# A graph layer with eight splits of the edges instead of six, and a reordered opening

## The chip, the cores and the metric

The kernel runs on one core of a Trainium2 chip. The profile names the core's engines: PE (TensorE, matrix products; PEld is its weight loading), DVE (VectorE), ACT (ScalarE), POOL (GpSimd) and SP (SyncE, which issues most transfers). Each engine runs its own instructions in the program's order and waits for the others by semaphores. The metric is device time in microseconds, from the first to the last instruction with what lies around them, median of the runs.

## The reference

One layer of message passing over 100,000 edges and 6,250 nodes, 128 features. `src` is random, `dst` is sorted.

```python
row, col = (edge_index[0], edge_index[1])          # src, dst
msg_in = jnp.concatenate([x[row], x[col], edge_attr], axis=-1)
h = msg_in @ W + b                                  # W: (384, 128)
mu = jnp.mean(h, axis=-1, keepdims=True)
var = jnp.mean(jnp.square(h - mu), axis=-1, keepdims=True)
h = (h - mu) * jax.lax.rsqrt(var + LN_EPS) * gamma + beta
msg = jax.nn.relu(h)
out = jax.ops.segment_sum(msg, row, num_segments=x.shape[0])
...
x = _layernorm(x + out, axis=-1)
```

## The kernel before

**Two passes, woven together.** Edges are worked in 782 tiles of 128, four tiles to a block (196 blocks, `q`). The first pass makes, for each edge, `edge_attr @ W[2D:]` (`features`, L943) plus the projected `x[dst]`, picked by a one-hot product from a window of 42 rows (`edges`, L960; the one-hot is `ohd`, L932). ACT copies the block from PSUM to `hs` and appends each edge's place in its node block (`evict`, L968 and L969, one L969 for each block). Then POOL scatters the rows into DRAM, one indirect DMA for each tile (`scatters`, L990), sorted by node block: node `n` belongs to block `n % 50`. Where a row goes is ranked by `places` on DVE and PE (L685 to L731, products L725) ahead of time.

**Splits.** The 782 tiles are cut into splits, each with its own DRAM tensor `sorted_d[s]` and a fixed room for each node block: `SPLITS` says (tiles, tiles of room for a node block, rows of the room that are never cleared, pieces in which it is ranked). What the scatters may leave empty is cleared by DMAs from `empty` ahead (`clear`, L431). Once a split is complete, the second pass reads it back by pairs of node blocks (`load_pair`, L1049 before). A pair of a split with room `k` has 2k *slots* (tiles of 128 sorted rows).

**What a pair does** (class `Pair`): a one-hot of the nodes (`ones`, L1106, DVE), its transposes (`turn`, PE L1118, copied by ACT in `turned`), the rows put into PSUM (`seed`), the node's own projection added by products (`pick`, L1145), squares and root (`square`, ACT L1154 and L1157), reciprocal and `msg` on DVE (`root` L1163, `scale` L1169: one `msg` instruction for each slot), the sum over edges by products into `pa` (`sums`, L1178), and the addition to `acc` (`add`, L1196). While tiles are still coming, the loop over blocks does a few pair steps in each (`work`, table `FLOW`); how many is set by `due`, which spreads a split's 25 pairs, four steps each, evenly over the blocks from its completion (plus `LAG`) to the next.

**The end.** The pairs of the last split (called x) can start only after the last scatter, and they also finish the nodes (`Finish`: the outer layer norm and the store). The order of steps there comes from a planner, `in_order`, a list scheduler with a table of ranks (`RANK`) and of ready times (`READY`) in its own units. To have less left, 8 of the 25 x pairs are halved: their first tiles of both node blocks are worked earlier, two pairs at a time, as four *units* (`UNITS`, class `Unit`, loads L1062, sums L1214, additions L1221). Before the change the units' rows lay in the last split's tensor: its first 68 tiles (`FULL`) had to be scattered, and `check_full` tested that these fill the first tile of each node block.

Of the kernel before, what the change touches and what calls it, by code (L numbers as in the profile page):

```python
# [8 lines left out]
F32 = mybir.dt.float32  # L9
# [4 lines left out]
ALU = mybir.AluOpType  # L14
# [71 lines left out]
def flat(t):  # L86
# [4 lines left out]
READY = {"u": 13.5, "x": 25.5, "pool": 24.5}  # L91
RANK = {"O": -1.5, "T": 0.4, "U": -3.2, "S": 0.3, "K": 4.4, "Q": 6.1, "R": -2.7, "V": 4.1, "C":
        7.1, "M": 9.0, "A": 8.9, "B": 10.6, "St": 12.6, "FQ": 15.6, "W": 9.5, "E": 25.4, "L":
        -13.2, "F": -6.8, "D": 14.0, "N": 1.9, "H": 5.3}
PACE = 2.6
LOOK = 0.04
# [30 lines left out]
def last_steps(old, units, halves, n):  # L127
# [42 lines left out]
    for i in range(n):  # L170
# [15 lines left out]
        steps["V", "x", i] = Step("DVE", 0.107, 0.09, [("R", "x", i)], rank("V"))  # L186
# [5 lines left out]
        if i == n - 1:  # L192
            last_pair(steps, i, ring, rank)
            continue
# [3 lines left out]
                                  takes=("y",) if i < n - 3 else (), gives=((("F", "x", i), "xs"),))  # L198
# [9 lines left out]
        if i == n - 2:  # L208
            steps["E0", "x", i] = Step("DVE", 0.3, 0.1, [("W", "x", i)], rank("E"))
            steps["E1", "x", i] = Step("ACT", 0.5, 0.1, [("W", "x", i)], rank("E"))  # L210
        else:
            steps["E", "x", i] = Step("POOL", 0.88, 0.06, [("W", "x", i)], rank("E"))
        if i < n - 3:
            steps["D", "x", i] = Step("SP", 0.4, 2.5, [("E", "x", i)], rank("D"),
# [4 lines left out]
def last_pair(steps, i, ring, rank):  # L219
# [4 lines left out]
    steps["N", "x", i] = Step("PE", 1.5, 0.2, [("H", "x", i), ("O", "x", i)], rank("N"),  # L224
# [82 lines left out]
def fast_path(ctx, tc, io, bad_d):  # L307
# [177 lines left out]
    def first_nodes(t0, t1):  # L485
        c = slice(t0, t1)
        nc.vector.tensor_scalar(sloc[:, c], src_i[:, c], 0.5, 1.0 / NB, op0=ALU.add, op1=ALU.mult)
        nc.vector.tensor_scalar(sloc[:, c], sloc[:, c], -0.5, MAGIC, op0=ALU.add, op1=ALU.add)
# [184 lines left out]
    def places(s, t0, T):  # L673
# [59 lines left out]
        if t0 + T == first_tile[-2] + FULL:  # L733
            check_full()
        yield

    def check_full():

        n = place_pool.tile([P, NB], F32, name="n_edges")
        nc.vector.tensor_scalar(n, room[-1], P - 1.5, None, op0=ALU.is_lt)  # L740
        red = place_pool.tile([P, 1], F32, name="red")
        nc.vector.tensor_reduce(red, n.unsqueeze(1), axis=AX.X, op=ALU.max)
        nc.vector.tensor_tensor(bad[:, 2:3], bad[:, 2:3], red, op=ALU.add)
# [122 lines left out]
    def edge_loads(q):  # L866
# [7 lines left out]
        for n in ([(0, g)] if q else [(i, 1) for i in range(g)]):  # L874
            c0, c1 = n[0] * PT * P, min((n[0] + n[1]) * PT * P, (TILES - t0) * P)
            nc.sync.dma_start(eT[:, c0:c1], io["eT"][:, t0 * P + c0:t0 * P + c1])
            if q == 0 and n[0] == 0:
                load_first(0)
                load_first(1)
                load_x(0, 1)  # L880
# [94 lines left out]
    full_scatters = []  # L975
# [3 lines left out]
    def scatters(n, tied):  # L979
# [7 lines left out]
        for k, (s, q, j) in enumerate(waiting[:n]):  # L987
# [8 lines left out]
            if first_tile[-2] <= t < first_tile[-2] + FULL:  # L996
                full_scatters.append(i.ins.name)
# [4 lines left out]
            if t >= first_tile[-2] + FULL:  # L1002
                tc.declare_no_dep(i.ins, group="halves", reason="see check_full")
                tc.add_to_no_dep_group("behind", i.ins)
# [39 lines left out]

    def load_pair(s, p):
# [3 lines left out]
        nc.sync.dma_start(flat(pair[:, :k, :]),  # L1049
                          dram_ap(sorted_d[s], p * k * P * ROW, [[k * ROW, P], [1, k * ROW]]))  # L1050
        loaded[s, p] = pair

    def load_unit(a, b):
# [7 lines left out]
        for j, p in ((0, a), (2, b)):  # L1061
            i = nc.sync.dma_start(flat(hl[:, j:j + 2, :]),  # L1062
                                  dram_ap(sorted_d[-1], p * 4 * P * ROW,
                                          [[2 * ROW, P], [1, 2 * ROW]]))
# [897 lines left out]
```

## Time and profile before

| | |
|---|---|
| median of 3 runs | 1337.93 us (1335.0 to 1340.36) |
| the profiled execution | 1336.07 us, span 1334.3 us |
| mean granted TensorE clock | 0.844 |
| PE, DVE, ACT, POOL busy | 72%, 66%, 56%, 61% |
| first and last scatter start | 10.54 us, 1236.62 us |

Read the busy shares as means over stages with different limits. A group row of the page gives line, engine, operation, tiles out and in, count, then busy time and mean duration, then the engine's idle time ahead of that group and what ended it. A row of a window gives its bounds and length, the busy time of each engine with the count of its instructions, and last the granted clock, the share of the DMA engines' time and GB/s. A timeline row gives start, duration, engine, line, operation and tiles, and in brackets the idle time before it and what ended that.

### The profile page before, as it was taken

The numbers are of one execution on the slowest core, as the hardware profiler recorded it, in microseconds if no ns is written. First come the engines' busy times: TensorE is split into PE (matmuls) and PEld (weight loads), VectorE is DVE, ScalarE is ACT, GpSimd is POOL, SyncE is SP. The second block draws the span as 40 slices with busy tenths as digits, with TensorE's granted clock in tenths as the row PEclk, the third lists the DMA queues.
The fourth block names the chain that finished last, engine by engine and source line by source line (L and its number), as shares of the span: only waits on it lengthen the run. The fifth ranks groups of instructions, "written<-read, shape, count | busy, mean of one in ns | idle before, by whom it ended". The sixth has DMA issues, their size and how long they took to land.

```text
span 1334.3 us, 27455 instructions
## 1 busy us (share of the span) xinstructions
PE 954.9 (72%) x8745; PEld 865.6 (65%) x8745; DVE 881.5 (66%) x2457; ACT 743.0 (56%) x3118; POOL 818.6 (61%) x900
## 2 busy tenths in 40 slices
PE   6554644544877877777877777777778777877796
PEld 5543643533766776666777677777778777767674
DVE  6756747734776767776677575565657666665797
ACT  4121321102555555555655556777669887777697
POOL 6656665666666666666666656666565565565087
PEclk7677775666888888898888888998899999998898
DMA  7876764544666655556567546666576665655263
GB/s 218 262 229 200 226 192 140 182 132 152 208 212 198 191 178 171 167 173 207 187 190 219 180 160 209 206 201 203 166 239 207 216 196 162 192 156 148 61 187 110
DMA packets 127676, 247.93 MB, mean 186 GB/s; under 512 B 47103, under 2 KB 62737, under 8 KB 127525
## 3 DMA queue, kind: packets, MB, share of 16 engines
q1 hardware_dynamic: 101635, 192.55, 48.1%
q0 software_dynamic: 25024, 52.85, 11.2%
q8 instruction: 70, 1.15, 0.4%
q10 hardware_dynamic: 866, 0.72, 0.2%
q14 instruction: 81, 0.66, 0.1%
HBM read 156.23 MB, written 89.80 MB: 184 GB/s over the span
## 4 chain that ended last, share of the span: by engine, by line
PE 47%; DVE 18%; issue 16%; ACT 10%; another core or an unknown queue 7%; DMA 1%; POOL 0%; SPq 0%; ACTq 0%; DVEq 0%; POOLq 0%
PE pa L1178 15%; PE sel L1145 11%; PE hp L943 9%; PE tr L1118 4%; DVE msg L1169 3%; DVE sc L689 3%; ACT sq L1154 3%; PE beside L725 2%; PE hp L960 2%; ACT hs L968 2%; ACT sel L1128 2%; DVE oh L685 1%; DVE ohe L1106 1%; DVE far L708 1%
## 5 line engine op out<-in xcount | busy, mean ns | idle before, releaser
L990 POOL DMA_INDIRECT sorted<-hs,place_i x782 | 756.8, 968 | 470.4 <-issue 199.5
L1178 PE MATMUL pa<-msg,ohe 128*128 128x130 f32 x1788 | 278.3, 309 | 51.9 <-issue 26.8
L1154 ACT ACTIVATE sq<-sel 128x128 f32<-128x128 f32 x866 | 228.3, 279 | 145.9 <-remote 47.5
L1145 PE MATMUL sel<-xa,ohn 128*128 128x128 bf16 x2760 | 227.2, 232 | 112.6 <-issue 58.6
L968 ACT COPY hs<-hp 128x512 f32<-128x512 f32 x194 | 113.0, 583 | 334.3 <-issue 106.8
L943 PE MATMUL hp<-w,eT 128*128 128x128 f32 x1548 | 261.8, 317 | 41.7 <-issue 27.5
L1178 PEld LDWEIGHTS pa<-msg,ohe 128*128 128x128 f32 x1788 | 249.9, 217 | 63.0 <-issue 31.7
L1145 PEld LDWEIGHTS <-ohn 128*128 128x128 bf16 x2850 | 195.7, 105 | 134.4 <-issue 125.7
L1169 DVE SCALAR_TENSOR_TENSOR msg<-sel,rstd,cut 128x128 f32<-128x128 f32 x920 | 260.5, 345 | 8.2
L943 PEld LDWEIGHTS hp<-w,eT 128*128 128x128 f32 x1548 | 231.9, 227 | 48.0 <-issue 32.7
L1154 ACT ACTIVATION_READ_ACCUMULATOR sq<-sel 128x1 f32 x866 | 181.3, 209 | 0.0
L1106 DVE TENSOR_TENSOR ohe<-hl,beside 128x1024 f32<-128x1024 f32 (+2 forms) x138 | 139.1, 1008 | 25.4 <-PE hp L960 7.9
L1122 ACT COPY ohn<-tr 128x1024 bf16<-128x1024 bf16 (+3 forms) x154 | 125.3, 814 | 35.3 <-PE tr L1118 11.0
L1128 ACT COPY sel<-hl 128x512 f32<-128x512 f32 (+1 forms) x225 | 127.7, 568 | 8.9 <-DVE msg L1169 6.2
L1196 DVE TENSOR_TENSOR acc<-acc,pa 128x260 f32<-128x260 f32 x124 | 51.9, 419 | 102.9 <-PE sel L1145 43.8
L1118 PE MATMUL tr<-ident_h,ohe 128*128 128x128 bf16 x910 | 84.6, 232 | 41.2 <-issue 34.3
L1163 DVE RECIPROCAL rstd<-std 128x4 f32<-128x4 f32 (+1 forms) x229 | 39.3, 172 | 95.1 <-ACT std L1157 53.6
L1118 PEld LDWEIGHTS <-ohe 128*128 128x128 bf16 x910 | 64.7, 105 | 53.4 <-issue 46.5
L960 PE MATMUL hp<-win,ohd 126*128 126x128 bf16 x770 | 87.5, 238 | 13.8 <-issue 11.7
L932 DVE TENSOR_SCALAR ohd<-db,part_w 128x512 bf16<-128x512 bf16 x192 | 70.0, 365 | 38.2 <-remote 21.6
L960 PEld LDWEIGHTS <-ohd 126*128 126x128 bf16 x770 | 68.2, 109 | 22.6 <-issue 16.1
L1157 ACT ACTIVATE std<-ss,eps 128x4 f32<-128x4 f32 (+1 forms) x229 | 68.1, 297 | 7.5
(249 smaller groups left out, 914.7 us busy)
## 6 DMA issues: line engine op xcount, KB each, us to landing
eT<-in_eT SPq DMA_DIRECT2D x96, 512.0 KB
hl<-sorted SPq DMA_DIRECT2D x75, 528.0 KB
db<-drel_d SPq DMA_DIRECT2D x96, 256.0 KB
sorted<-empty SPq DMA_DIRECT2D x100, 198.0 KB
sorted<-hs,place_i POOLq DMA_INDIRECT x782
hl<-sorted SPq DMA_DIRECT2D x42, 264.0 KB
hl<-sorted SPq DMA_DIRECT2D x25, 396.0 KB
sorted<-empty SPq DMA_DIRECT2D x50, 132.0 KB
```

The costliest lines, as they stand in the source:

```text
L943: pe(nc.tensor.matmul(hp[:, j, :], eT[:, at], w[:, 2, :], start=j == 0, stop=False, skip_group_check=True), 4)
L960: pe(nc.tensor.matmul(hp[:, j, :], oh[:3 * WN, at], win[:3 * WN, :], start=False, stop=j == m - 1, skip_group_check=True))
L968: nc.scalar.copy(hs[:, :m, 0:D], hp[:, :m, :])
L990: i = nc.gpsimd.indirect_dma_start(out=sorted_d[s][:, :], out_offset=bass.IndirectOffsetOnAxis(ap=place_i[:parts, t:t + 1], axis=0), in_=h ...
L1106: nc.vector.tensor_tensor(self.ohe[:, :k, :], self.rows()[:, :k, D:D + 1].to_broadcast([P, k, P]), row_bc(iota_p, k), op=ALU.is_equal)
L1118: pe(nc.tensor.transpose(tr[:, j, :], half[:, j0 + j, 1::2], ident_h))
L1122: nc.scalar.copy(self.ohn[:, :self.k, :], self.tr[:, :self.k, :])
L1128: copy(self.sel[g][:, :m, :], self.rows()[:, j0:j0 + m, 0:D])
L1145: pe(nc.tensor.matmul(sel[:, j, :], self.ohn[:, j0 + j, :], xa[:, b, i * D:(i + 1) * D], start=False, stop=j == m - 1 and i == 2, skip_gro ...
L1154: nc.scalar.activation(sq[:, j, :], self.sel[g][:, j, :], AF.Square, accum_out=ss[:, j:j + 1])
L1169: nc.vector.scalar_tensor_tensor(self.msg[:, j0 + j, 0:D], self.sel[g][:, j, :], rstd[:, j:j + 1], cut, op0=ALU.mult, op1=ALU.max)
L1178: pe(nc.tensor.matmul(self.pa[:, h, :], self.ohe[:, j, :], self.msg[:, j, :], start=(j == h), stop=(j == k - 2 + h)), 4)
```

## The change

Six splits become eight. The last 78 tiles with two tiles of room for each node block become two splits of 36 and 34 tiles with one tile of room each; the earlier ones are cut anew, to 712 tiles in place of 704. The units read the split of 36 tiles; a halved pair then reads the split of 34, and the 17 other x pairs read one slot for each of their node blocks from both, by two loads. `check_full` and the dependences that it needed are gone. `due` spreads the pairs of six splits (before: five), and `LAG` is 6.

```diff
-SPLITS = [(168, 4, 320, [8, 16, 28, 40, 38, 38]),
-          (168, 4, 320, [42, 42, 42, 42]),
-          (168, 4, 320, [42, 42, 42, 42]),
+SPLITS = [(160, 4, 320, [8, 16, 28, 36, 36, 36]),
+          (160, 4, 320, [40, 40, 40, 40]),
           (120, 3, 192, [40, 40, 40]),
+          (112, 3, 192, [38, 37, 37]),
           (80, 2, 128, [40, 40]),
-          (78, 2, 128, [39, 29, 10])]
-FULL = 68
+          (80, 2, 128, [40, 40]),
+          (36, 1, 48, [36]),
+          (34, 1, 48, [34])]
...
-READY = {"u": 13.5, "x": 25.5, "pool": 24.5}
+READY = {"u": -20.0, "x": 22.5, "pool": 21.5}
-RANK = {"O": -1.5, "T": 0.4, "U": -3.2, "S": 0.3, "K": 4.4, "Q": 6.1, "R": -2.7, "V": 4.1, "C":
+RANK = {"O": -1.8, "T": 0.4, "U": -4.4, "S": 7.2, "K": 6.0, "Q": 6.1, "R": 0.0, "V": 6.3, "C":
...
-        if t0 + T == first_tile[-2] + FULL:
-            check_full()
...
+    def rows(out, s, p):
+        k = 2 * SPLITS[s][1]
+        nc.sync.dma_start(flat(out),
+                          dram_ap(sorted_d[s], p * k * P * ROW, [[k * ROW, P], [1, k * ROW]]))
...
         for j, p in ((0, a), (2, b)):
...
-            for name in full_scatters:
-                tc.add_manual_dep(i.ins, name, written, reason="rows of the full tiles")
+            rows(hl[:, j:j + 2, :], n_split - 2, p)
...
     def load_rest(p):
-        if p not in HALVES:
-            return load_pair(n_split - 1, p)
         pair = late["blk"].tile([P, KMAX, ROW], F32, name="hl", bufs=4)
-        nc.sync.dma_start(flat(pair[:, :2, :]),
-                          dram_ap(sorted_d[-1], (p * 4 + 2) * P * ROW,
-                                  [[2 * ROW, P], [1, 2 * ROW]]))
+        for j, r in enumerate((n_split - 1,) if p in HALVES else (n_split - 2, n_split - 1)):
+            rows(pair[:, 2 * j:2 * j + 2, :], r, p)
...
-    pairs = [(s, p) for s in range(n_split - 1) for p in range(NB // 2)]
+    pairs = [(s, p) for s in range(n_split - 2) for p in range(NB // 2)]
...
-    LAG = 5
+    LAG = 6
-    due = [(first_tile[s] // PT + LAG, (s - 1) * 2 * NB) for s in range(1, n_split)]
+    due = [(first_tile[s] // PT + LAG, (s - 1) * 2 * NB) for s in range(1, n_split - 1)]
...
-                clear_pairs(s + 1, 1 if slots > NB // 2 else 2)
+                clear_pairs(s + 1, 1 if slots > NB // 2 else -(-NB // 2 // slots))
```

The opening is written in another order:

```diff
     turning(6)
+    load_first(0)
     edge_loads(0)
...
+    first_sloc(0, n0)
     spread = signs()
-    turning(4)
+    turning(1)
     window_rows()
+    nc.gpsimd.tensor_copy(ident_h, ident)
+    nc.gpsimd.tensor_copy(ident_f16, ident)
     weights_beside(1)
...
-    run(first)
-    run(near_x, 2)
-    run(first)
+    run(near_x)
+    run(first, 2)
+    run(near_x)
     features_half(0, 0, 0)
     run(near_x, 2)
     hot_first(0, 0, 2 * P)
-    nc.gpsimd.tensor_copy(ident_f16, ident)
     features_half(0, 0, 1)
     run(near_x)
     hot_first(0, 2 * P, 4 * P)
-    hot_first(1, 0, 2 * P)
+    edges_half(0, 0)
+    evict_half(0, 0)
     run(first)
     paired(0, n0)
     run(first)
-    edges_half(0, 0)
-    evict_half(0, 0)
...
-    hot_first(1, 2 * P, PT * P, nc.vector)
+    hot_first(1, 0, PT * P, nc.vector)
...
-    bases([0])
     run(second)
+    bases([0])
```

`first_sloc` is the first instruction of `first_nodes`, taken out of it; `rows` is the load that three places had each for itself. The rest of the diff gives the planner a possible sharing of the last step between POOL and ACT, which is not used (`SHARED = ()`), and other weights.

**Where instructions stand.** POOL at the very start, from the signs of the weights (`w`) to the first scatter (`sorted`); `ohd` is the one-hot of the first blocks. Before:

```order
L467 TENSOR_TENSOR w<-w,sgn 128x128
L1356 TENSOR_SCALAR minus_h<-ident 128x128
L1357 CAST ident_h<-ident 128x128
L467 TENSOR_TENSOR w<-w,sgn 128x128
L836 TENSOR_SCALAR ohd<-first_i,part 128x256
L1367 CAST ident_f_133<-ident 128x128
L836 TENSOR_SCALAR ohd<-first_i,part 128x256 x2
L990 DMA sorted_71<-hs_174,place_i 67584x132 x4
```

And POOL at the same place now:

```order
L1340 CAST ident_h<-ident 128x128
L1341 CAST ident_f_135<-ident 128x128
L474 TENSOR_TENSOR w<-w,sgn 128x128
L1350 TENSOR_SCALAR minus_h<-ident 128x128
L474 TENSOR_TENSOR w<-w,sgn 128x128
L838 TENSOR_SCALAR ohd<-first_i,part 128x256 x2
L990 DMA sorted_71<-hs_180,place_i 65536x132 x4
```

Both conversions of `ident` moved ahead of the signs, and two one-hots in place of three stand ahead of the first scatter.

DVE in the middle, about block 100, before; `ohd` opens a block, `msg` stands for four slots, `oh`, `pos` and `place_i` belong to the ranking:

```order
L932 TENSOR_SCALAR ohd<-db,part_w 128x512
L1106 TENSOR_TENSOR ohe<-hl,beside 128x1024
L729 TENSOR_REDUCE pos<-beside 128x40
L731 SCALAR_TENSOR_TENSOR place_i<-pos,bkt 128x40
L1163 RECIPROCAL rstd<-std 128x4
L1169 SCALAR_TENSOR_TENSOR msg_2242<-sel,rstd,cut 128x128 x4
L932 TENSOR_SCALAR ohd<-db,part_w 128x512
L1196 TENSOR_TENSOR acc<-acc,pa 128x260
L685 TENSOR_TENSOR oh<-bkt_h,beside 128x1000
L1163 RECIPROCAL rstd<-std 128x4
L1169 SCALAR_TENSOR_TENSOR msg_2242<-sel,rstd,cut 128x128 x4
```

DVE at the same block now:

```order
L933 TENSOR_SCALAR ohd<-db,part_w 128x512
L1096 TENSOR_TENSOR ohe<-hl,beside 128x1024
L720 TENSOR_TENSOR far<-oh,beside 128x1000
L726 TENSOR_TENSOR sc<-sc,oh 128x480
L726 TENSOR_TENSOR sc<-sc,oh 128x520
L726 TENSOR_TENSOR sc<-sc,oh 128x480
L726 TENSOR_TENSOR sc<-sc,oh 128x520
L1153 RECIPROCAL rstd<-std 128x4
L1159 SCALAR_TENSOR_TENSOR msg_2252<-sel,rstd,cut 128x128 x4
L1186 TENSOR_TENSOR acc<-acc,pa 128x260
L1153 RECIPROCAL rstd<-std 128x4
L1159 SCALAR_TENSOR_TENSOR msg_2252<-sel,rstd,cut 128x128 x4
```

A block that held four slots beside the ranking holds eight here; the ranking itself has stayed.

DVE at the end, from the last whole pairs to the units; `ohe<-hl` is the one-hot of a pair, `ohe<-oh` and `ohe<-sc` those of the units, whose rows lie in the former ranking tiles, and sums come back by `acc<-acc,pa`. Before:

```order
L1169 SCALAR_TENSOR_TENSOR msg_2243<-sel,rstd,cut 128x128 x4
L1196 TENSOR_TENSOR acc<-acc,pa 128x260
L1163 RECIPROCAL rstd<-std 128x4
L1169 SCALAR_TENSOR_TENSOR msg_2241<-sel,rstd,cut 128x128 x4
L1196 TENSOR_TENSOR acc<-acc,pa 128x260
L1163 RECIPROCAL rstd<-std 128x4
L1169 SCALAR_TENSOR_TENSOR msg_2242<-sel,rstd,cut 128x128 x4
L1196 TENSOR_TENSOR acc<-acc,pa 128x260 x2
L1106 TENSOR_TENSOR ohe<-oh,beside 128x512 x2
L1106 TENSOR_TENSOR ohe<-sc,beside 128x512 x2
L1163 RECIPROCAL rstd<-std 128x4
L1169 SCALAR_TENSOR_TENSOR msg_2243<-sel,rstd,cut 128x128 x4
```

DVE at that place now:

```order
L1153 RECIPROCAL rstd<-std 128x4
L1159 SCALAR_TENSOR_TENSOR msg_2253<-sel,rstd,cut 128x128 x4
L1096 TENSOR_TENSOR ohe<-oh,beside 128x512
L1096 TENSOR_TENSOR ohe<-hl,beside 128x512
L1186 TENSOR_TENSOR acc<-acc,pa 128x260
L1153 RECIPROCAL rstd<-std 128x4
L1159 SCALAR_TENSOR_TENSOR msg_2254<-sel,rstd,cut 128x128 x4
L1153 RECIPROCAL rstd<-std 128x4
L1159 SCALAR_TENSOR_TENSOR msg_2252<-sel,rstd,cut 128x128 x4
L1096 TENSOR_TENSOR ohe<-hl,beside 128x512
L1186 TENSOR_TENSOR acc<-acc,pa 128x260
L1153 RECIPROCAL rstd<-std 128x4
```

The units' one-hots stood behind the last addition of the whole pairs; the first of them now stands among three pairs that are still to be summed.

More of the change, by code (lines that the diff above doesn't have):

```diff
@@ L192, in last_steps @@
         if i == n - 1:
-            last_pair(steps, i, ring, rank)
+            last_pair(steps, i, k, ring, rank)
             continue
@@ L1048, in load_pair @@
         pair = late["blk"].tile([P, KMAX, ROW], F32, name="hl", bufs=4)
-        nc.sync.dma_start(flat(pair[:, :k, :]),
-                          dram_ap(sorted_d[s], p * k * P * ROW, [[k * ROW, P], [1, k * ROW]]))
+        rows(pair[:, :k, :], s, p)
         loaded[s, p] = pair
@@ L1356, in fast_path @@
     nc.gpsimd.tensor_scalar(minus_h, ident, -1.0, None, op0=ALU.mult)
-    nc.gpsimd.tensor_copy(ident_h, ident)
     run(near_x)
@@ L1409, in fast_path @@
     halved(n0, 12 * n0)
+    run(second)
     bases([0])
-    run(second)
     features(2)
@@ L1565, in fast_path @@
     s, n = n_split - 1, NB // 2
-    x = [Pair(s, p, p in HALVES) for p in range(n)]
+    x = [Pair(s, p, 2 if p in HALVES else 4) for p in range(n)]
     f = [Finish(2 * p, 2) for p in range(n)]
@@ L1617, in ends @@
     def ends(i):
-        for j in range(FN):
+        for j in range(1 if i in SHARED else FN):
             f[i].end_block(j, nc.gpsimd)
```

61 lines of the change are left out of this document (27 added, 34 removed).

## The prediction

> **What bounds the kernel now.** I read the page first, then the stages by windows, then the two ends by the timeline.
>
> ```profile
> span 1334.3 us, 27455 instructions
> ...
> PEclk7677775666888888898888888998899999998898
> ...
> PE 47%; DVE 18%; issue 16%; ACT 10%; another core or an unknown queue 7%; DMA 1%; POOL 0%; SPq 0%; ACTq 0%; DVEq 0%; POOLq 0%
> ...
> L990 POOL DMA_INDIRECT sorted<-hs,place_i x782 | 756.8, 968 | 470.4 <-issue 199.5
> ```
>
> No engine fills the span, and the chain that ended last is spread over PE, DVE, ACT and issue time: the kernel is a pipeline of blocks of four edge tiles, and the question is how long one block takes under which load. The scatters alone are not the floor. Back to back they start every 1.26 us (rows below), 5.06 us for the four of a block, and 782 of them would need 990 us, where they are spread over 1226 us.
>
> ```profile
> 1201.17 0.96 POOL L990 DMA_INDIRECT sorted<-hs,place_i  x1 [0.30 <-issue]
> 1202.43 0.96 POOL L990 DMA_INDIRECT sorted<-hs,place_i  x1 [0.30 <-issue]
> ```
>
> So I cut the middle where the rate of pair work changes (blocks 57, 131, 161, 181, 195). First fence: busy time by engine; second: the evictions' L969 copies, one for each block; third: the `msg` instructions L1169, one for each slot, by which I mean one tile of 128 sorted rows that a pair works on.
>
> ```profile
> 354.50:813.10 458.60, 352.88 (x3216) 323.59 (x3215) 323.73 (x834) 256.69 (x1073) 286.88 (x296) 0.85 0.60 188
> 813.10:1003.50 190.40, 149.59 (x1550) 139.75 (x1550) 108.64 (x329) 137.31 (x586) 116.15 (x121) 0.92 0.64 203
> 1003.50:1134.60 131.10, 103.63 (x1187) 97.89 (x1185) 89.13 (x278) 107.69 (x478) 77.62 (x81) 0.99 0.63 198
> 1134.60:1224.30 89.70, 69.72 (x729) 64.58 (x728) 53.93 (x172) 65.61 (x289) 53.13 (x56) 0.94 0.52 160
> ```
>
> ```profile
> 354.50:813.10 458.60, 14.90 (x74) 0.85 0.60 188
> 813.10:1003.50 190.40, 6.11 (x30) 0.92 0.64 203
> 1003.50:1134.60 131.10, 4.00 (x20) 0.99 0.63 198
> 1134.60:1224.30 89.70, 2.80 (x14) 0.94 0.52 160
> ```
>
> ```profile
> 354.50:813.10 458.60, 100.03 (x356) 0.85 0.60 188
> 813.10:1003.50 190.40, 55.58 (x199) 0.92 0.64 203
> 1003.50:1134.60 131.10, 45.21 (x158) 0.99 0.63 198
> 1134.60:1224.30 89.70, 26.33 (x93) 0.94 0.52 160
> ```
>
> Call the stages A to D. A block takes 6.20, 6.35, 6.56 and 6.41 us with 4.8, 6.6, 7.9 and 6.6 slots. The load rises by two thirds from A to C and the block by 6%: the pair work is mostly, not wholly, laid into gaps. PE is busy 77, 79, 79 and 78% of each stage, while its granted clock goes from 0.85 to 0.99. A also holds the ranking of edges (`places`), which ends before B.
>
> **The change, part by part.** *Eight splits.* Slots in the splits that are worked beside the tiles go from 25 pairs x (8+8+8+6+4) = 850 to 25 x (8+8+6+6+4+4) = 900; what follows after the last tile stays at 4 units of 4 and 84 slots. So 50 slots and 25 more pairs go into the middle, while tiles and scatters stay 782. Price of one slot: from B to C (6.556 - 6.347) / (7.90 - 6.63) = 0.164 us. With it, a block without ranking is 6.347 + 0.164 x (slots - 6.63); at A's 4.81 slots that gives 6.05, so ranking costs 0.15 us a block. D by this line is 6.35, measured 6.41. 50 slots then cost 50 x 0.164 = **+8.2 us**. Lower bound: from A to B 1.82 slots cost 0.15 us with ranking gone, 0.08 each, 4.1 us. Upper bound: the stage before pair work, where six blocks took 29.9 us, gives (6.347 - 4.98) / 6.63 = 0.206, 10.3 us.
>
> ```profile
> 252.80:282.70 29.90, 18.34 (x83) 14.09 (x84) 13.72 (x39) 3.91 (x13) 19.99 (x21) 0.56 0.34 104
> 252.80:282.70 29.90, 1.21 (x6) 0.56 0.34 104
> ```
>
> I take B to C, the step between two stages without ranking that are nearest to the new loads. The load is also dealt out anew: by the table of due times, blocks 86 to 116 get 6.7 slots each (5 before), 144 to 164 7.5, 164 to 184 5.0 (before some 7), 184 to 195 7.7. On a straight line only the sum of slots counts; the first of these places is where the line may bend (first rival).
>
> *The end.* The units' rows now lie in a split of their own, complete nine blocks before the last tile. Their steps move between those of the last whole pairs.
>
> ```profile
> 1227.70 1.75 SPq L1062 DMA_DIRECT2D oh<-sorted  x4
> ...
> 1236.62 0.88 POOL L990 DMA_INDIRECT sorted<-hs,place_i  x1 [0.30 <-issue]
> ...
> 1238.80 0.32 SPq L1075 DMA_DIRECT2D hl<-sorted  x1
> ```
>
> ```profile
> 1228.63 0.29 DVE L1691 COPY beside<-beta 128x128 f32<-128x128 f32 x1
> ...
> 1245.07 1.28 DVE L1106 TENSOR_TENSOR ohe<-oh,beside 128x512 f32<-128x512 f32 x2
> ...
> 1250.56 0.18 DVE L1163 RECIPROCAL rstd<-std 128x4 f32<-128x4 f32 x1 [3.02 <-ACT std L1157]
> ...
> 1258.66 0.41 DVE L1106 TENSOR_TENSOR ohe<-hl,beside 128x256 f32<-128x256 f32 x1
> ...
> 1262.07 0.17 DVE L1596 RECIPROCAL rstd<-std 128x2 f32<-128x2 f32 x1 [1.47 <-ACT std L1591]
> ```
>
> ```profile
> 1228.60:1258.70 30.10, 22.13 (x210) 19.76 (x208) 20.27 (x67) 20.99 (x97) 4.71 (x5) 0.85 0.27 81
> 1258.70:1324.20 65.50, 61.39 (x564) 48.23 (x565) 62.44 (x275) 56.85 (x308) 51.13 (x89) 1.00 0.53 154
> ```
>
> The units' rows were asked for at 1227.7 and their first one-hot came at 1245.1, since DVE had five old pairs in front; the last scatter was issued at 1236.6 and its rows asked for at 1238.8, yet the last pairs began at 1258.7. In those 30.1 us DVE worked 20.3 and waited 9.8, mostly for the root of a single pair in flight. From 1258.7 on DVE is busy 62.4 of 65.5 us: there only work counts, and it stays the same. With units and old pairs interleaved I let half of the 9.8 us go. Against it, the first last pair now starts behind all the units' sums; its wait of 1.47 us was partly covered by them, and 1.4 us more of DVE work (four additions) leaves that place. Net **-3.5 us**; at best -8.5, at worst +1. The last pairs' rows now come by two loads from two tensors for 17 of 25 pairs; one such issue takes 0.32 us of SP, 17 x 0.32 = 5.4 us more within 65, and the loads run four pairs ahead: nothing, or about 1 us at the first four pairs if the lead is missing.
>
> *The opening.* SP issues `first_i` one place earlier, POOL's conversion of `ident_f` leaves its place between two one-hots, and a third one-hot leaves POOL for DVE.
>
> ```profile
> 2.44 0.43 SPq L876 DMA_DIRECT2D eT<-in_eT  x1
> ...
> 7.34 0.94 POOL L836 TENSOR_SCALAR ohd<-first_i,part 128x256 bf16<-128x256 int32 x1 [1.06 <-DMA first_i<-in_dstC]
> ...
> 8.22 0.29 POOL L1367 CAST ident_f<-ident 128x128 f16<-128x128 f32 x1
> 8.50 1.85 POOL L836 TENSOR_SCALAR ohd<-first_i,part 128x256 bf16<-128x256 int32 x2
> 8.57 0.35 PE L787 MATMUL beside<-far,ident_f 128*128 128x136 f16 x3 [1.09 <-DVE bkt L519]
> ...
> 8.93 0.67 PE L854 MATMUL hp<-first_x,ohd 128*128 128x128 bf16 x6
> ...
> 9.46 0.17 DVE L794 SCALAR_TENSOR_TENSOR place_i<-pos,bkt 128x8 int32<-128x8 f32 x1
> ...
> 10.54 1.23 POOL L990 DMA_INDIRECT sorted<-hs,place_i  x1 [0.20 <-DVE sloc L487]
> ```
>
> The first scatter stood behind 1.85 us of one-hots. Now: first one-hot at 7.34 - 0.43 = 6.9, two of 0.93 end at 8.8. PE puts six edge products (0.67) ahead of the ranking's six; they start at 7.85, the ranking's at 8.5 as before, so the places come at 9.6 and the scatter at some 9.75: **-0.8 us**. The three fewer warming products of PE and the smaller moves lie beside this path and cost nothing. The third one-hot goes to DVE behind the update of `room`, off this path. Bounds 0 (the next wait, for the window tables, eats it) and -1.2.
>
> *Small work.* The test of full tiles (three DVE instructions) goes, two tests of room (five each) come.
>
> ```profile
> L813 DVE SCALAR_TENSOR_TENSOR lo<-n_edges,lo 128x50 f32<-128x50 f32 x6 | 1.3, 212 | 0.2
> ```
>
> At 0.21 us that is +1.5 us of DVE, in stages where it is 57 to 71% busy: nothing. The middle also gets 50 more clears and 25 more pair loads on SP, 75 x 0.32 = 24 us of issue over 930, and 7.6 MB more (8,000 more cleared rows and 6,400 more read, 528 bytes each), 47 us of traffic at D's 160 GB/s. The DMA engines are 52 to 64% busy in A to D and loads run ahead of use, so I count nothing; without that cover it would be up to those 47 us.
>
> Sum: 8.2 - 3.5 - 0.8 = +3.9 us on the profiled execution's 1336.07, that is 1340.0. This execution lies 1.9 us below the median of the runs, 1337.93, inside their spread of 1335.0 to 1340.4; I leave the sum at 1340. A measurement of this kernel tells about 0.5%, 6.7 us, from no change.
>
> **Rivals.** *Slower: the dense stage with ranking beside it.* Blocks 86 to 116 get B's load and still A's ranking, which no stage of the profile has.
>
> ```profile
> 354.50:813.10 458.60, 25.15 (x182) 17.10 (x182) 0.85 0.60 188
> ```
>
> Ranking's products L725 take PE 25.15 / 74 = 0.34 us a block. B's 4.99 + 0.34 = 5.33 us in my 6.50 would be 82% of PE, where no stage passes 79%. If 78.5% is what these dependences allow, the block takes 6.79, 30 x 0.29 = 8.7 us more: 1340.0 + 8.7 = 1349. It decides once that block is above 6.65. For it: the even shares of PE. Against it: 94% of PE in the last pairs (61.39 of 65.50).
>
> *Faster: the slots disappear in the gaps and the end closes.* The slots cost 2 us or less (half of the lower bound 4.1), and DVE's 9.8 us shrink by the full 8.5: 1336.07 + 2 - 8.5 - 0.8 = 1329. For it: the clock rose with each load in the rows above, so PE's old work got cheaper as new work came. Against it: C and D are longer than B at a higher clock.
> The Trainium skill ("TensorE: Matmul & The Clock Gate", Part 1) says that a monitor gates TensorE's clock to half and that sustained activity of about 3.4 us releases it. By that rule the denser blocks 86 to 116 would pay nothing for the ranking's products, and this rival gains; the granted clocks 0.85, 0.92 and 0.99 agree with its direction.
>
> *The end gives nothing*: the order is set by a table, and a wait for another root may stand where one for the old pairs stood. 8.2 - 0.8 = +7.4, 1343.5, still within the bound.
>
> **How the numbers follow.** The forecast, with the end that gives nothing, 0.45 (1334 to 1345); the dense stage 0.30 (1345 to 1356); the slots absorbed 0.22 (1323 to 1332); 0.03 for something slower that I don't see. So faster 0.23, same 0.45, slower 0.32. The range 1329 to 1351 leaves out the lower half of the fast case (0.1) and the upper part of the slow one (0.1).
>
> **What the profile after would show.** The scatter's first start near 9.75. Blocks 86 to 116 at 6.5 us (6.8 or more: first rival; 6.3: second). Blocks 164 to 184 near 6.1. DVE's wait between the copy of `beta` and the first last pair at about 5 us instead of 9.8, and that stretch 26 to 27 us instead of 30. From there to the end 75.6 us as before. Wrong would be: a scatter that waits for clears, since two small splits clear 25 pairs in nine blocks; or last pairs that wait for their second load.

## The result and the profile after

| | before | changed |
|---|---|---|
| median of 13 runs, us | 1337.93 (1331.4 to 1348.7) | 1347.64 (1344.6 to 1357.7) |
| ratio to before, 95% interval | | 1.007 (1.0049 to 1.0091) |
| profiled execution: span, us | 1334.3 | 1345.9 |
| first scatter starts, us | 10.54 | 12.35 |
| last eviction (block 195), us | 1224.2 | 1238.3 |
| from there to the end, us | 110.1 | 107.6 |

The changed kernel is 0.7% slower. That is inside the stated range of 1329 to 1351, but the forecast was 1340 and "no change". The page of the changed kernel: its span, its granted clock, the chain that ended last, and the scatters' group (busy time, mean ns of one, idle time before them).

```profile
span 1345.9 us, 28552 instructions
...
PEclk8767777766788988999999988989999877999999
...
PE 42%; DVE 21%; issue 15%; ACT 12%; another core or an unknown queue 6%; DMA 3%; POOL 1%; SPq 0%; ACTq 0%; DVEq 0%; POOLq 0%
...
L990 POOL DMA_INDIRECT sorted<-hs,place_i x782 | 756.8, 968 | 485.4 <-issue 197.6
```

The same chain, with more DVE in it, and the same 782 scatters of 968 ns; POOL waits 15 us longer between them. (In these rows "issue" is idle time for which the profile shows no wait.) Next the stages that the new table of due times loads differently, blocks 86 to 116, 116 to 131 and 164 to 184. First two fences: the kernel before, evictions (one a block), then slots; last two: the changed kernel.

```profile
533.60:718.70 185.10, 17.46 (x30) 0.86 0.60 188
718.70:812.60 93.90, 8.72 (x15) 0.82 0.58 180
1023.60:1154.80 131.20, 11.53 (x20) 0.97 0.61 191
```

```profile
533.60:718.70 185.10, 40.60 (x144) 0.86 0.60 188
718.70:812.60 93.90, 20.61 (x74) 0.82 0.58 180
1023.60:1154.80 131.20, 44.03 (x153) 0.97 0.61 191
```

```profile
540.40:731.00 190.60, 17.48 (x30) 0.96 0.65 205
731.00:829.90 98.90, 8.73 (x15) 0.91 0.59 182
1038.70:1166.60 127.90, 11.54 (x20) 0.86 0.61 185
```

```profile
540.40:731.00 190.60, 56.36 (x200) 0.96 0.65 205
731.00:829.90 98.90, 26.13 (x91) 0.91 0.59 182
1038.70:1166.60 127.90, 30.36 (x108) 0.86 0.61 185
```

Blocks 86 to 131 took 10.5 us longer for 73 slots more (0.14 each). Blocks 164 to 184 gave back 3.3 us for 45 slots fewer (0.07 each). The granted clock followed the load, from 0.86 to 0.96 in blocks 86 to 116 and from 0.97 to 0.86 in 164 to 184. That agrees with the direction of the rule in the Trainium skill ("TensorE: Matmul & The Clock Gate", Part 1), but the faster clock did not pay for the slots.

The opening: SP's issues, then PE, then POOL.

```profile
2.42 0.43 SPq L379 DMA_DIRECT2D first_i<-in_dstC  x1
2.89 0.43 SPq L878 DMA_DIRECT2D eT<-in_eT  x1
```

```profile
8.19 0.76 PE L849 MATMUL hp<-w,eT 128*128 128x128 f32 x2 [1.74 <-DMA eT<-in_eT]
...
9.38 0.85 PE L856 MATMUL hp<-first_x,ohd 128*128 128x128 bf16 x6
10.02 0.54 PE L789 MATMUL beside<-far,ident_f 128*128 128x136 f16 x3
```

```profile
7.54 1.83 POOL L838 TENSOR_SCALAR ohd<-first_i,part 128x256 bf16<-128x256 int32 x2 [1.59 <-DMA first_i<-in_dstC]
12.35 1.22 POOL L990 DMA_INDIRECT sorted<-hs,place_i  x1 [2.98 <-DVE sloc L494]
```

PE now waits for the edge features, whose load is issued behind `first_i` (8.19; 6.53 before), and the ranking's products stand behind them and behind the first edges' (10.02; 8.57 before). `first_i` itself was issued 0.5 us earlier, but its first one-hot could start at 7.54 instead of 7.34.

The end: DVE's copy of `beta`, the one-hot of the first last pair, and the two stretches that these divide (busy time of PE, PE loads, DVE, ACT, POOL).

```profile
1244.77 0.28 DVE L1683 COPY beside<-beta 128x128 f32<-128x128 f32 x1
...
1272.12 0.42 DVE L1096 TENSOR_TENSOR ohe<-hl,beside 128x256 f32<-128x256 f32 x1
```

```profile
1244.70:1272.10 27.40, 20.80 (x211) 17.23 (x207) 21.28 (x69) 20.54 (x97) 4.54 (x5) 1.00 0.30 92
1272.10:1336.00 63.90, 60.54 (x561) 48.38 (x561) 60.95 (x271) 57.36 (x307) 50.07 (x86) 1.00 0.53 156
```

The stretch is 27.4 instead of 30.1, with 6.1 us of DVE's waits instead of 9.8, and from the first last pair to the end it is 73.8 instead of 75.6. Between the last eviction and the copy of `beta` 2.1 us came on top (6.5 instead of 4.4). The two signs of being wrong that the prediction named did not show: no wait of a scatter is put down to a clear, and the wait of DVE for rows of the last pairs is 0.6 us in all.

### The profile page after: what moved, and what is told of

Read it like the earlier page. It is cut to its first block, busy times and chain, and to the rows that moved or that the text cites. A ratio compares the mean times of both kernels' runs of the same rounds, so it can differ in the third digit from the quotient of the medians.

```text
span 1345.9 us, 28552 instructions
## 1 busy us (share of the span) xinstructions
PE 958.1 (71%) x9052; PEld 872.6 (65%) x9052; DVE 917.8 (68%) x2596; ACT 778.3 (58%) x3293; POOL 817.4 (61%) x899
## 3 DMA queue, kind: packets, MB, share of 16 engines
q1 hardware_dynamic: 109183, 200.16, 49.6%
## 4 chain that ended last, share of the span: by engine, by line
PE 42%; DVE 21%; issue 15%; ACT 12%; another core or an unknown queue 6%; DMA 3%; POOL 1%; SPq 0%; ACTq 0%; DVEq 0%; POOLq 0%
PE pa L1168 12%; PE sel L1135 10%; PE hp L944 9%; DVE msg L1159 5%; ACT sq L1144 4%; PE tr L1108 4%; DVE sc L701 3%; ACT sel L1118 2%; PE hp L961 2%; PE beside L737 2%; ACT ohn L1112 2%; DMA sorted<-hs,place_i 2%; DVE ohe L1096 2%; ACT hs L969 1%
## 5 line engine op out<-in xcount | busy, mean ns | idle before, releaser
L1144 ACT ACTIVATE sq<-sel 128x128 f32<-128x128 f32 x916 | 241.8, 280 | 138.2 <-PE sel L1135 39.5
L1135 PE MATMUL sel<-xa,ohn 128*128 128x128 bf16 x2898 | 228.6, 229 | 104.5 <-ACT sel L1118 47.6
L1159 DVE SCALAR_TENSOR_TENSOR msg<-sel,rstd,cut 128x128 f32<-128x128 f32 x966 | 274.7, 345 | 9.1
L1135 PEld LDWEIGHTS <-ohn 128*128 128x128 bf16 x3000 | 199.3, 103 | 123.9 <-issue 101.7
L1144 ACT ACTIVATION_READ_ACCUMULATOR sq<-sel 128x1 f32 x916 | 191.9, 210 | 0.0
L1096 DVE TENSOR_TENSOR ohe<-hl,beside 128x1024 f32<-128x1024 f32 (+3 forms) x163 | 149.6, 918 | 12.8 <-PE sel L1135 11.6
L1112 ACT COPY ohn<-tr 128x512 bf16<-128x512 bf16 (+2 forms) x179 | 134.2, 749 | 38.7 <-issue 11.0
L1118 ACT COPY sel<-hl 128x512 f32<-128x512 f32 (+1 forms) x250 | 136.9, 548 | 8.5 <-issue 4.7
L1153 DVE RECIPROCAL rstd<-std 128x4 f32<-128x4 f32 (+1 forms) x254 | 43.8, 172 | 132.7 <-ACT std L1147 79.9
L1186 DVE TENSOR_TENSOR acc<-acc,pa 128x260 f32<-128x260 f32 x149 | 62.0, 416 | 78.2 <-PE pa L1168 24.1
L961 PE MATMUL hp<-win,ohd 126*128 126x128 bf16 x770 | 88.0, 240 | 25.9 <-issue 16.6
L1108 PE MATMUL tr<-ident_h,ohe 128*128 128x128 bf16 x960 | 88.9, 227 | 24.4 <-issue 12.3
L933 DVE TENSOR_SCALAR ohd<-db,part_w 128x512 bf16<-128x512 bf16 x192 | 69.7, 363 | 38.8 <-remote 31.9
L1147 ACT ACTIVATE std<-ss,eps 128x4 f32<-128x4 f32 (+1 forms) x254 | 75.4, 297 | 8.2
```

The lines of the kernel that those rows point to most:

```text
L961: pe(nc.tensor.matmul(hp[:, j, :], oh[:3 * WN, at], win[:3 * WN, :], start=False, stop=j == m - 1, skip_group_check=True))
L1096: nc.vector.tensor_tensor(self.ohe[:, :k, :], self.rows()[:, :k, D:D + 1].to_broadcast([P, k, P]), row_bc(iota_p, k), op=ALU.is_equal)
L1108: pe(nc.tensor.transpose(tr[:, j, :], half[:, j0 + j, 1::2], ident_h))
L1112: nc.scalar.copy(self.ohn[:, :self.k, :], self.tr[:, :self.k, :])
L1118: copy(self.sel[g][:, :m, :], self.rows()[:, j0:j0 + m, 0:D])
L1135: pe(nc.tensor.matmul(sel[:, j, :], self.ohn[:, j0 + j, :], xa[:, b, i * D:(i + 1) * D], start=False, stop=j == m - 1 and i == 2, skip_gro ...
```

## The experiments

The runs fell on several chips. On some the kernel before takes 1336 to 1353 (called 1340 chips below; the result above is from such a one), on others 1093 to 1095 (1094 chips). Each ratio is to runs of the kernel before on the same chip; times of the two kinds are never compared as an effect of an edit. So an expectation that was written for a 1340 chip and met a 1094 chip could not be tested there in its figures.

**The opening undone.** The whole opening of the kernel before in the changed kernel (1094 chip).

```diff
-    load_first(0)
     edge_loads(0)
...
-    turning(1)
+    turning(4)
...
-    edges_half(0, 0)
-    evict_half(0, 0)
+    hot_first(1, 0, 2 * P)
     run(first)
     paired(0, n0)
     run(first)
+    edges_half(0, 0)
+    evict_half(0, 0)
```

> The changed kernel with the opening of the kernel before put back (order of loads, warming products, where the one-hots and the casts stand); splits, end and table of due times stay changed. Theory: the first scatter came 1.8 us late (12.35 instead of 10.54) because PE waited for the edge features that are now loaded behind first_i, and this delay passes on undiminished, since the scatters set the pace before the pair work. Then the first scatter is back at 10.5, block 20 is 1.8 us earlier than in the changed kernel, and the time is about 1345.8 (ratio to before 1.0055). Rival: slack later in the kernel takes the delay in; then the first scatter is back at 10.5 and the time still 1347.6 (1.007).

1093.06, ratio 0.9992 (0.998 to 1.0005). The first scatter was not back at 10.5, as both theory and rival had it, but came at 11.92, since POOL's first one-hot waited for `first_i` until 8.30 and the cast of `ident_f`, which the ranking needs, stood behind it.

**Only the load put back** (1094 chip).

```diff
-    load_first(0)
     edge_loads(0)
...
-                load_x(0, 1)
+                load_first(0)
                 load_first(1)
+                load_x(0, 1)
```

> The changed kernel with one thing of its opening undone: SP issues first_i behind the first load of edge features again. The rest of the new order on PE, POOL and DVE stays. Theory (the moved load is what was wrong with the opening): PE's first feature products start near 6.6 instead of 8.19 and the first scatter at 10.0 to 10.6. Rival (the products of the first edges ahead of the ranking's, or PE's lower clock after three warming products fewer, cost it): first scatter still at 11.5 or later.

1093.40, ratio 1.0003 (0.9989 to 1.0018). PE's feature products start at 6.24: the late load was the cause of that wait. But the first scatter is at 11.59, as the rival had it: the first edges' products wait for POOL's one-hot, and the ranking's stand behind them.

**Seven splits, with the new and with the old opening** (1094 chips; the first of them on two chips).

```diff
-SPLITS = [(160, 4, 320, [8, 16, 28, 36, 36, 36]),
-          (160, 4, 320, [40, 40, 40, 40]),
-          (120, 3, 192, [40, 40, 40]),
-          (112, 3, 192, [38, 37, 37]),
-          (80, 2, 128, [40, 40]),
+SPLITS = [(168, 4, 320, [8, 16, 28, 40, 38, 38]),
+          (168, 4, 320, [42, 42, 42, 42]),
+          (168, 4, 320, [42, 42, 42, 42]),
+          (128, 3, 192, [43, 43, 42]),
           (80, 2, 128, [40, 40]),
           (36, 1, 48, [36]),
           (34, 1, 48, [34])]
```

> The changed kernel with seven splits, 168, 168, 168, 128, 80, 36 and 34 tiles: the new opening and the new end stay, and 850 slots are worked beside the tiles as before, instead of 900. Theory: the 50 slots cost about 0.16 to 0.2 us each, and the ranking's pieces, which are those of before again, take away the longer pause of the scatters at block 35 (14.5 us there instead of 12.2): 1347.6 - 8.2 - 2.3 = 1337, within 1335 to 1339. Rival (the loss is not in the slots but in the end's two loads a pair and in its new order): 1344 or more.

> Seven splits as in the run with them, and the opening of before: what is left of the change is the end alone, with the last split in 36 and 34 tiles. Theory: 1.8 us below the run with seven splits and the new opening, 1335 (ratio to before 0.998), by the 2.5 us that the end gained in the changed kernel's trace. Rival (the end gives nothing or costs): 1338 or more.

> The kernel with seven splits and 850 slots again, for a chip where the kernel before takes some 1340 to 1350. There the theory (the loss is the 50 slots, 8 of 9.4, and neither the opening nor the end) gives 1.001, within 0.999 to 1.003; the rival (the end or the opening) 1.005 to 1.007. Where the kernel before takes 1094 it is 1.0065 again.

1.0065 (1.0049 to 1.0081), 1.0071 (1.0055 to 1.0088), and again 1.0065 (1.0042 to 1.0088). Fifty slots fewer than the changed kernel, and on these chips slower. The next run shows the changed kernel there.

**The changed kernel itself on a 1094 chip.**

> The changed kernel itself, unaltered, beside the four runs before, in which the kernel before took 1093 instead of 1338 and its scatters ran with no pauses. Theory: where the scatters run back to back (1.26 us each, 782 of them), they set the pace up to the last one and hide the 50 slots; the change then gives the same time as before, ratio 0.998 to 1.002; where the kernel before takes some 1338, its scatters pause for the pair work and the ratio is 1.005 to 1.009 again. Rival (the extra slots cost their 8 us or more anywhere): 1.007 in both.

1092.41, ratio 0.9985 (0.9972 to 0.9997). The same program, 0.7% slower on one kind of chip, is not slower on the other. Its page and its evictions for blocks 86 to 116, 116 to 131, 131 to 144, 164 to 184 and 184 to 195:

```profile
L990 POOL DMA_INDIRECT sorted<-hs,place_i x782 | 756.9, 968 | 243.0 <-issue 96.8
```

```profile
419.30:593.00 173.70, 17.42 (x30) 0.93 0.74 234
593.00:672.10 79.10, 8.65 (x15) 0.96 0.73 225
672.10:722.80 50.70, 7.43 (x13) 1.00 0.91 288
827.60:920.60 93.00, 11.48 (x20) 0.94 0.81 249
920.60:982.10 61.50, 6.27 (x11) 0.97 0.67 207
```

Each scatter takes the same 968 ns, but POOL waits 243 us between them instead of 485: mostly they start every 1.263 us, 5.05 a block. The evictions do not keep that pace: 5.79 us a block in 86 to 116, then 3.90 in 131 to 144. What links the two is how far the engines run ahead of the scatters, from a block's eviction to its first scatter: 31.9 us at block 86, 11.0 at 131, 26.1 at 144, 24.8 at 195. The dense blocks beside the ranking are paid out of this lead, and light blocks fill it up again. The program bounds the lead on both sides: there are eight buffers `hs` for evicted blocks, and from block 12 on the scatters of a block are tied behind products of the next (`scatters(len(waiting) - PT, True)`), so that about one block is the least. On the 1340 chip the lead of the changed kernel is 6 to 9 us at each of these blocks up to 184 and 10.6 at 195, where a block takes 6.2 to 6.6. So it is near its least: the scatters wait for products (the largest such sums below: us in total, times, longest), and every block's length counts.

```profile
POOL sorted L990 <- PE sel L1135: 54.6, 59, 1.6
POOL sorted L990 <- PE pa L1168: 50.6, 52, 2.6
```

The kernel with seven splits shows the same from the other side; its blocks 86 to 116, 164 to 184 and 184 to 195 by evictions, then by slots:

```profile
420.80:576.30 155.50, 17.44 (x30) 0.90 0.73 227
821.90:929.20 107.30, 11.52 (x20) 1.00 0.82 253
929.20:993.50 64.30, 6.25 (x11) 1.00 0.69 201
```

```profile
420.80:576.30 155.50, 40.59 (x144) 0.90 0.73 227
821.90:929.20 107.30, 44.79 (x156) 1.00 0.82 253
929.20:993.50 64.30, 26.35 (x93) 1.00 0.69 201
```

Blocks 86 to 116 with 4.8 slots take 5.18 instead of 5.79, and that gains nothing, since the lead is full (31 to 32 us at blocks 86 to 144) and the scatters set the pace. Blocks 164 to 184, with 7.8 slots instead of 5.4, take 5.37 instead of 4.65, blocks 184 to 195, with 8.5 instead of 7.6, take 5.85 instead of 5.59, and the lead at the last eviction is 14.7 instead of 24.8. The last scatter starts at 1009.5 here and at 1008.3 in the changed kernel, so up to it the scatters cost both the same. But the end is reckoned from the last eviction, and from there it is as long in both (107.0 and 107.1): the time follows the last eviction, 993.6 against 982.2. So the lead matters twice on these chips: the scatters pause where it runs out, and what is left of it at the last eviction shortens the end. The kernel with seven splits has the 850 slots of the kernel before and still takes 0.7% more. So something else in the change costs here, the new dealing of the load or the end; which, and whether it costs on a 1340 chip too, no run shows.

**More pairs, and the load dealt evenly** (1094 chip).

```diff
-          (160, 4, 320, [40, 40, 40, 40]),
+          (80, 2, 128, [40, 40]),
+          (80, 2, 128, [40, 40]),
```

> The changed kernel with its second split of 160 tiles made two of 80 (two tiles a block each): the same 900 slots in 25 more pairs, with 25 more loads and as many more clears. Theory (slots are what costs, not pairs): the same as the changed kernel within 3 us. Rival (the loads, clears and the fixed steps of a pair cost, 9.8 us for 25 pairs in the two traces): 10 us more.

1121.65, 1.0253 (1.0232 to 1.0273). My expectation overlooked that the due table moves with the splits: the 200 slots of the first split now had to be done in 20 blocks, 46 to 66, beside the ranking.

```profile
215.80:360.00 144.20, 11.55 (x20) 0.91 0.74 234
```

That is 7.21 us a block; the lead fell to 4.6 at block 86, and the scatters had to wait: the last one starts at 1039.7 instead of 1008.3. The run says nothing about pairs against slots; it shows where the lead runs out.

```diff
+    due = [(46, 0), (86, 100), (116, 193), (144, 304), (164, 389), (184, 504), (197, 600)]
```

> The changed kernel with another table of due times, which deals the same 900 slots out evenly, 6.2 a block from block 86 on, instead of 6.7, 5.4, 7.5, 5.0 and 7.7. Theory (the blocks that have 7 and more slots, or 6.7 beside the ranking, run over what fits in the gaps, while the light ones don't give it back): 2 to 4 us less than the changed kernel. Rival (only the sum of the slots counts): the same within 2 us.

1100.21, 1.006 (1.0042 to 1.0078): 8 us more than the changed kernel, the opposite of the theory, and not the rival's "same" either: with one sum of slots, where they stand sets the time on this chip. The lead at the last eviction is 18.8 instead of 24.8, and blocks 184 to 195 take 6.16 us (67.8 for 11) instead of 5.59, with as many slots. Why these take longer is open.

**Fifty slots more** (1094 chip).

```diff
-          (120, 3, 192, [40, 40, 40]),
+          (120, 4, 256, [40, 40, 40]),
```

> The changed kernel with one number changed: the split of 120 tiles gets 4 tiles a block instead of 3, so that its 25 pairs have 8 slots each instead of 6. 50 slots more, no pair, load or clear more (the loads are longer); they fall into blocks 116 to 144, which then have 7.1 slots instead of 5.4. Theory where the kernel before takes some 1340 to 1350 (a slot costs 0.16 wherever it falls): 8 more than the changed kernel, ratio 1.013, and blocks 116 to 144 longer by 0.3. Rival (light blocks take slots in at no cost): the changed kernel's 1.007. Where the kernel before takes 1094: hidden behind the scatters, 0.9985 as the changed kernel, unless 7 slots are more than a block of 5.06 holds.

1105.88, 1.0109 (1.0086 to 1.0131): 13.5 us more than the changed kernel, 0.27 a slot. They were not hidden; the expectation's "unless" came true. Blocks 116 to 131, with 7.2 slots:

```profile
593.60:681.30 87.70, 8.65 (x15) 0.96 0.72 229
```

5.85 us a block. The lead, 6.4 us at block 131, was used up there, the scatters fell behind, and at the last eviction it was 11.6 instead of 24.8 (in a profiled execution that lies 5.5 us above the median).

**The opening mended, and the kernel before for its profile** (1340 chips).

```diff
-    load_first(0)
     edge_loads(0)
...
-    edges_half(0, 0)
-    evict_half(0, 0)
     run(first)
     paired(0, n0)
     run(first)
+    edges_half(0, 0)
+    evict_half(0, 0)
     features_half(0, 1, 0)
```

> The changed kernel with two places of its opening mended: first_i is loaded behind the first edge features again, and PE does the ranking's products ahead of the first edges' products, which wait for POOL's one-hots. Theory: the first scatter then waits for neither a late load nor for products of the edges ahead of the ranking, and comes at 10.0 to 10.6 instead of 12.0; where the scatters set the pace, the time falls by as much, to about 1.5 below the changed kernel (ratio to before 0.997 where before takes 1094, 1.0055 where it takes 1338). Rival (POOL's wait for first_i decides it, whatever PE does): first scatter at 11.5 or later and no gain.

1362.06, ratio 1.007 (1.0044 to 1.0096). PE and POOL:

```profile
7.42 0.54 PE L789 MATMUL beside<-far,ident_f 128*128 128x136 f16 x3
...
9.24 0.82 PE L856 MATMUL hp<-first_x,ohd 128*128 128x128 bf16 x6 [0.95 <-POOL ohd L838]
```

```profile
10.78 1.22 POOL L991 DMA_INDIRECT sorted<-hs,place_i  x1 [0.53 <-ACT hs L863]
```

The first scatter is as early as in the kernel before on this chip (10.84), and the loss is the same 0.7%. So the opening is not the main part of what made the change slower; its 1.8 us lie below what the interval can tell. The mended version is no faster than either kernel.

> The kernel before, unaltered, for its profile beside those of the changed kernel on a chip where it takes some 1094. Theory: the 850 slots are hidden there as the 900 are, the last scatter starts at 1008 to 1011 in both (1008.3 in the changed kernel), and what the changed kernel gained there, 0.15% or 1.6, is its end: from the last scatter to the end 83 to 85 here, 81.0 in the changed kernel. Rival (the end gives nothing): 81 here too. If the chip is one where it takes 1338, its blocks from 57 on take 6.2 to 6.7 again and the table by stages is that of the first profile within 1%.

> The kernel before, unaltered, once more for its profile on a chip where it takes some 1094. Theory: its end is as long as in the two profiles at hand, 110 from the last eviction (L968) to the end instead of 107 in the changed kernel, and this is all that sets them apart there, so its last eviction comes at 983 to 985 (982.2 in the changed kernel) in spite of 50 slots fewer, because its blocks 144 to 195 carry more slots (7.2 and 7.6 a block) than the changed kernel's 164 to 184 (5.4). Rival (the 50 slots cost there too): last eviction at 976 or earlier and an end of 115. If it falls on a chip where it takes 1340 to 1360: the stages of the two earlier profiles again, blocks 86 to 131 at 6.2 to 6.35.

Both fell on 1340 chips (1352.5 and 1336.6, ratios 0.9996 and 0.998), so there is no profile of the kernel before on a 1094 chip. They give three profiles of the kernel before and two of the changed one (the first, and the one with the mended opening) by stages on 1340 chips, us a block from the evictions:

| blocks | slots before | us before, three profiles | slots changed | us changed, two profiles |
|---|---|---|---|---|
| 50 to 57 | 2.9 | 6.29, 6.25, 6.17 | 4.0 | 6.51, 6.55 |
| 57 to 86 | 4.7 | 6.19, 6.32, 6.17 | 5.0 | 6.23, 6.29 |
| 86 to 116 | 4.8 | 6.17, 6.38, 6.14 | 6.7 | 6.35, 6.48 |
| 116 to 131 | 4.9 | 6.26, 6.22, 6.41 | 6.1 | 6.60, 6.63 |
| 131 to 144 | 6.6 | 6.35, 6.51, 6.40 | 5.3 | 6.19, 6.39 |
| 144 to 164 | 7.2 | 6.42, 6.48, 6.43 | 7.4 | 6.42, 6.61 |
| 164 to 184 | 7.7 | 6.56, 6.66, 6.63 | 5.4 | 6.39, 6.33 |
| 184 to 195 | 6.0 | 6.30, 6.50, 6.34 | 7.5 | 6.51, 6.54 |

From block 50 to 195 the mean is 920.4 before (914.1, 930.7, 916.5) and 929.9 changed (923.9, 935.8): +9.4 us, as much as the medians differ by (9.7). But that is a difference of means of three and of two executions, and those of the kernel before alone lie 16.6 apart; the first profiles of the two kernels give 9.8, the second ones 5.1. So the profiles say where the loss lies, and its size there only roughly. Up to block 50 the executions differ more among themselves (310.1, 318.0, 316.7 before; 314.4, 309.9 changed) than between the kernels. The end from the last eviction is 110.1, 110.3, 109.5 before and 107.6, 110.3 changed: the gain of the first pair did not come again. Its last part, from the first last pair on, did (75.6 in all three before; 73.8 and 74.1), but DVE waited 8.4 us ahead of it in the second changed profile instead of 6.1.

## Why the prediction was right, and where it failed

- *The range held by its width.* The middle was +3.9, the medians differ by 9.7. In the first pair of profiles all three terms came out worse than forecast, blocks 50 to 195 by 1.6 us, the end by 1.0 and the opening by 2.6, and 2.5 more came up to block 50 for which no term stood. The range was wide enough for that; that it held is in part luck.
- *The slots: right way, a little small; the cause is not shown.* Forecast +8.2 (0.164 each, bounds 4.1 to 10.3). Blocks 50 to 195 measured +9.4 on the mean of the profiles and +9.8 in the first pair, 0.19 to 0.20 each if all of it is put down to the 50 slots. No run on a 1340 chip shows that it is: the same stages also carry 25 more pairs with their loads and clears, and another dealing of the load. The stages show where the extra comes from. Blocks 86 to 116 cost what the line says or less (6.50 forecast, 6.35 and 6.48), blocks 116 to 131 more (6.4 by the line, 6.60 and 6.63), and lighter blocks do not give it back: blocks 164 to 184 were to take 6.1 and took 6.39 and 6.33, some 5 us over the 20. The step that failed is "On a straight line only the sum of slots counts": with some 3 to 5 slots a block of the 1340 chip still takes 6.1 to 6.6 (50 to 57 before, with 2.9 slots: 6.17 to 6.29), though the six blocks without pair work took 4.98 each. Why is open.
- *The end: right way in the first pair, too large.* Forecast -3.5; measured -2.5 there, and nothing in the second changed profile (110.3). DVE's waits went from 9.8 to 6.1 (about 5 forecast) and the stretch is 27.4 (26 to 27 forecast); the second time they were 8.4, and the stretch 29.8. The stretch ahead of the copy of `beta`, which I did not look at, took 2.1 back, and the last pairs gave 1.8 (1.5 the second time), which I had at nothing.
- *The opening: wrong.* Forecast -0.8, with a first scatter near 9.75; it came at 12.35, +1.8. The step that failed: "PE puts six edge products (0.67) ahead of the ranking's six; they start at 7.85". It forgot that two feature products stand in front on PE and wait for `eT`, whose load was moved back by the very issue I counted as a gain. And the gain wasn't there in this profile: the one-hot started at 7.54, against 7.34 to 7.42 in the three of the kernel before. (On the 1094 chips it did start earlier with the new order, at 6.95 to 7.52 in six profiles against 7.84 and 8.30, and the first scatter came no earlier for it.) The runs with the load alone and with both places mended show both waits.
- *The sum.* 9.8 - 2.5 + 4.3 for the first 50 blocks (314.4 - 310.1) is the 11.6 of the two spans. Of the 4.3 the opening explains 1.8; the rest lies within what executions differ by.
- *The rivals.* The time fell where I had put the dense stage, 1345 to 1356, but by its own mark it did not happen: blocks 86 to 116 stayed below 6.65. On the 1094 chips the same blocks do fall behind the scatters (5.79 against 5.18 with 4.8 slots), and that is paid from the lead. That the change can cost nothing is what the 1094 chip showed (0.9985); the lead accounts for it there. The granted clock rose there too (0.92 in the mean of these runs, 0.90 in those of the kernel before on the same chip), and no run separates the two. I gave "same" 0.45 because I took half a gain at the end and a whole one at the opening for sure enough to halve the cost of the slots.

Not separated by a run on a 1340 chip: whether the 9.4 us belong to the 50 slots, to the 25 pairs with their loads and clears, or to the new dealing of the load (one of the two things that can have cost 0.7% with 850 slots on the 1094 chips). The kernels with seven splits, with nine, with 50 slots more and with the even load have times on 1094 chips alone.

## What to carry to other kernels

Between a producer and a queue that drains at its own pace lies a lead, and extra work can be hidden only as long as the lead lasts: read it off as the distance from a block's last producer step to its drain, stage by stage, before pricing an added instruction. Where there is such a lead, as on the 1094 chips here, put dense stages where light ones follow before the end. And when a load is issued earlier, look at what is issued later for it and who waits for that at the head of an in-order engine.

## What the hardware showed that I had not expected

One chip needed 18% less time than another for the same program (1093.5 and 1337.9 us for the kernel before), though instructions off PE took as long: in the changed kernel a scatter 968 ns on both, the squares L1144 280 and 279 ns. PE's products were somewhat slower on the 1340 chip (the picks L1135 229 and 223 ns in the mean, at granted clocks of 0.868 and 0.916). The DMA packets were not: those of the main queue took 49.6% of 1345.9 us and 60.9% of 1089.3, that is 668 and 663 us. What differs stands around PE. ACT's square waits for the pick L1135. On the 1340 chip (the changed kernel, PE then ACT) and on the 1094 chip (the same):

```profile
868.29 0.79 PE L1135 MATMUL sel<-xa,ohn 128*128 128x128 bf16 x9
...
871.07 0.28 ACT L1144 ACTIVATE sq<-sel 128x128 f32<-128x128 f32 x1 [2.83 <-remote]
```

```profile
653.05 0.66 PE L1135 MATMUL sel<-xa,ohn 128*128 128x128 bf16 x9
...
653.75 0.28 ACT L1144 ACTIVATE sq<-sel 128x128 f32<-128x128 f32 x1 [1.03 <-PE sel L1135]
```

The first starts 1.99 us after PE's last recorded product, the second 0.04. Over all such waits behind 300 us and before the end phase the mean is 0.7 us (some 54 of them) on the one and 0.04 (13) on the other, while DVE starts 0.03 us behind ACT's root on both. PE itself stands still, too. Its waits in two stretches of 80 scatters each from about block 165 on (us in total, times, longest), first the 1340 chip, then, complete, the 1094 chip:

```profile
PE pa L1168 <- issue: 6.8, 5, 2.4
...
PE sel L1135 <- issue: 5.7, 9, 1.1
```

```profile
PE pa L1168 <- DVE acc L1186: 9.7, 14, 2.0
PE tr L1108 <- ACT ohn L1112: 2.8, 4, 1.8
```

On the one, 17.6 of the 126 us are pauses of PE for which the profile shows no wait ("issue", 21 of them); on the other there are none in 101 us. In the end phase the two chips agree again: such waits of ACT are 0.04 to 0.10, and from the copy of `beta` to the end it is 101.1 and 100.7 us. So it comes and goes with the scatter phase. Whether PE's products there end later than its records say, or the news of them arrives late, and what holds PE up, the profile does not tell.
